# Layer 1: the second-level result goes up to the first level as float32 products on the two 64-row parts of the PE array

## The chip, the cores and the metric

The kernel runs on one core of a Trainium2 chip. The time is the device time of one execution in microseconds (us), as a median of several executions. The engines named below are PE (matrix products; its weight loads are listed apart as PEld), DVE (vector), ACT (scalar), POOL (GpSimd) and SP, whose queue issues the DMA transfers. SBUF is the on-chip memory of 128 partitions; PSUM holds the sums that PE writes, in banks.

## What is computed

The network has four layers, each `x = x + conv(group_norm(x))`, on 32 images of 96 channels and 56 x 56 pixels in float32. The change lies in layer 1, a wavelet convolution:

```python
def _L1_conv_ref(x, base_w, base_b, base_scale, wconv_w, wscale):
    ...  # 3 levels of a 2x2 Haar transform of x; at each level a depthwise
    ...  # 5x5 convolution of the four bands, scaled; then from the lowest
    ...  # level up: the inverse transform adds a level's low band to the
    ...  # level above; the base 5x5 convolution of x is added at the end
x = x + _L1_conv_ref(_gn(x), ...)
```

The kernel folds a level's transform, convolution and inverse transform into one depthwise filter on that level's low band. So there are three depthwise products: at full size (level 1, which also has the base convolution in it), on 2 x 2 sums (level 2) and on 4 x 4 sums (level 3). The result of level 3 is spread over 2 x 2 points and added to level 2, and the result of level 2 is spread and added to level 1. This last step is what the change touches.

## The kernel before

Layer 1 works channel by channel, two channels (a pair) per turn of its main loop, 48 pairs. A channel is held for all 32 images at once. Rows and a phase of the columns lie on 112 partitions, the upper and the lower half of the image (h = 0, 1) are two tiles, each with 14 columns of 32 images, 448 elements per partition. A halo of 16 rows fills partitions 112 to 127. A depthwise convolution along rows is then a product with a banded 128 x 112 matrix, one for each of three column shifts (sizes 448, 416 and 416).

The steps of a pair, each for the pair named (`i` is the pair that is finished, `nxt` the next one, `far` the one after), with the lines of the profile:

- `normal(far, j, h)`: DVE normalises a half image, L872 and L873.
- `matrices1`, `matrices2`: ACT brings loaded matrices into order, L748 and L776; the loads into `raw` have been issued by SP.
- `lowest1(nxt)`: eight weight loads and products on four 32-column strips of the array make the 2 x 2 sums (L887), ACT copies them to `x2` (L889). `lowest2(nxt)` makes the 4 x 4 sums likewise (L895, L897).
- `level3(nxt)`: five products on two 64 x 64 parts of the array (L903), and two ACT copies into `c3` (L904, L905).
- `level2(nxt, j)`: three products (L912) and one that adds `c3`, spread by the constant `up2` (L913), in one PSUM tile of 128 partitions x 224; partitions 0 to 55 belong to the upper half image, 64 to 119 to the lower. Then, for each half, ACT writes a rounded copy in the type float32r (L918), and DVE writes what the rounding left out (L919): the high part lies on partitions 0 to 55 of `c2`, the low part on partitions 64 to 119, so that one product over 128 partitions adds both.
- `level1(i, j, h)`: takes a PSUM tile `pf` (a pool of four), `coarse` adds the spread `c2` of this half by two products in float32r with weights `up1r` over all 128 rows (L930, 224 columns each, one for each column phase n), `fine` adds the three shifted products in float32 (L924), and DVE adds the residual into `y` (L943). After h = 1 the SP queue stores `y` (L950).

The pair 0 does `fine` in advance, in `begin`, and `coarse` last. PE, DVE, ACT and SP run their instructions in the order in which the code issues them. That order is written out by hand in the main loop:

```python
            do(lowest1, nxt)
            ...
            do(level1, i, 0, 0)
            do(lowest2, nxt)
            ...
            do(level1, i, 0, 1)
            do(level3, nxt)
            ...
            do(level1, i, 1, 0)
            do(level2, nxt, 0)
            do(level2, nxt, 1)
            do(matrices2, far, 1)
            do(level1, i, 1, 1)
```

On PE a turn is therefore: L887, L930, L924, L895, L930, L924, L903, L930, L924, L912, L913, L912, L913, L930, L924. From the twelfth pair on the SP queue also gets transfers for layer 2 (L1106, whole groups of 16 channels at a time; L1113 for the last 16 channels) among the loads (L736, L739: images; L766 to L768: matrices; L783: factors of the norm).

Of the kernel before, what the change touches and what calls it, by code (L numbers as in the profile page):

```python
# [10 lines left out]
F32 = mybir.dt.float32  # L11
BF16 = mybir.dt.bfloat16
F32R = mybir.dt.float32r
I16 = mybir.dt.int16
AF = mybir.ActivationFunctionType
ALU = mybir.AluOpType
# [4 lines left out]
B, C, H, W = 32, 96, 56, 56  # L21
# [8 lines left out]
W4 = W // NPH  # L30
HH = H // 2
PH = HH * NPH
# [596 lines left out]
NK = 3  # L629
LEN = 2 * (HH + HALO) - 1  # L630
MIDL = HH + HALO - 1
KW = 5
# [118 lines left out]
def shifts(n, ks):  # L751


    for d in sorted(range(-(ks // 2), ks // 2 + 1), key=abs):
        yield ks // 2 + d, slice(max(0, -d), n - max(0, d)), slice(max(0, d), n + min(0, d))
# [32 lines left out]
def layer1(ctx, tc, w, y0, left, made, norm, t1, t2, t3, y1, k2, behind):  # L788
# [4 lines left out]
    nc = tc.nc  # L793
    cp = ctx.enter_context(tc.tile_pool(name="l1c", bufs=1, reuse_waits="tile"))
# [3 lines left out]
    pfine = ctx.enter_context(tc.tile_pool(name="l1pf", bufs=4, space=PSUM, reuse_waits="tile"))  # L798
    psum = ctx.enter_context(tc.tile_pool(name="l1p", bufs=4, space=PSUM, reuse_waits="tile"))
    N2, N3 = W4 // 2, W4 // 2  # L800

    def constant(name, shape):
        t = cp.tile(shape, F32, tag=name, name=name)
        nc.sync.dma_start(t, w[name])
        return t

    def rounded(name, shape):

        t = cp.tile(shape, F32R, tag=f"{name}r", name=f"{name}r")
        nc.scalar.copy(t, constant(name, shape))  # L810
        return t

    NF = 3
    sets = [None] * NF
    for i in reversed(range(NF)):
        sets[i] = {
            name: cp.tile(shape, dtype, tag=f"{name}{i}", name=f"{name}{i}") for name, shape, dtype in (
                ("T3", [128, 64 * KW], F32), ("T2", [128, 2, NK, 128], F32), ("raw2", [128, 2, NK * PH], F32), ("c2", [128, 2, 2, N2, B], F32R),
                ("c3", [128, N3, B], F32))}
    for d in sets:  # L820
        for t in d.values():
            nc.gpsimd.memset(t.bitcast(F32) if t.dtype == F32R else t, 0.0)

    def load(i):

# [81 lines left out]
    def level2(st, j):  # L907


        ps = psum.tile([128, N2, B], F32, tag="w", name="pc2")  # L910
        for n, (k, to, of) in enumerate(shifts(N2, NK)):
            nc.tensor.matmul(ps[:, to], st["T2"][:, j, k, :], st["x2"][:, j, of], start=(n == 0), stop=False)  # L912
        nc.tensor.matmul(ps, up2[:, j, :], st["c3"], start=False, stop=True)  # L913
        n = PH // 2
        for h in range(2):
            high, low = (st["c2"][64 * i : 64 * i + n, j, h] for i in range(2))
            v = ps[64 * h : 64 * h + n]
            nc.scalar.copy(high, v)  # L918
            nc.vector.tensor_tensor(low, v, high, ALU.subtract)  # L919

    def fine(st, j, h, first):
        ps = st["pf"][j, h]
        for n, (k, to, of) in enumerate(shifts(W4, NK)):
            nc.tensor.matmul(ps[:PH, to], st["T"][j][:, h, k, :], st["x"][:, j, h, of],  # L924
                             start=first and n == 0, stop=not first and n == NK - 1)

    def coarse(st, j, h, first):
        ps, rows = st["pf"][j, h], slice(128 if first else PH)
        for n in range(2):
            nc.tensor.matmul(ps[rows, n::2, :], up1[:, h, n, rows], st["c2"][:, j, h],  # L930
                             start=first and n == 0, stop=not first and n == 1)

    def level1(st, j, h):
        if h == 0:
            st["y"] = io.tile([PH, 2, B, W4], F32, tag="y", name="y", bufs=3)
        if st["i"]:
            st["pf"][j, h] = pfine.tile([128, W4, B], F32, tag="f", name="pc1")
            coarse(st, j, h, True)
            fine(st, j, h, False)
        else:  # L940
            coarse(st, j, h, False)
        ps = st["pf"][j, h]
        nc.vector.scalar_tensor_tensor(  # L943
            st["y"][:, h], ps[:PH].rearrange("p q b -> p b q"), st["nr"][j][:PH, 2 * B : 2 * B + 1], st["X"][j][:PH, h],
            ALU.add, ALU.add)
        if h == 1:
            c = 2 * st["i"] + j
            if c >= C - GR:
                k2.straight(c, st["y"], 0)
            nc.sync.dma_start(y1[c // GR][c % GR].rearrange("(h p) b q -> p h (b q)", h=2),  # L950
                              st["y"].rearrange("p h b q -> p h (b q)"))
            if c >= C - GR:
                k2.straight(c, st["y"], 1)

    def begin(st):
        for j in range(2):
            matrices1(st, j)
        for j in range(2):
            matrices2(st, j)
        both = cp.tile([128, 2, 2 * B + 1], F32, tag="nr0", name="nr0")  # L960
        made.spread(both, pick, psum.tile([128, 2, 2 * B + 1], F32, tag="w", name="pr0"))
        st["nr"] = [both[:, j, :] for j in range(2)]
        for j in range(2):
            for h in range(2):
                normal(st, j, h)
                st["pf"][j, h] = pfine.tile([128, W4, B], F32, tag="f", name="pc1")
                fine(st, j, h, True)
# [3 lines left out]
    def do(step, i, *args):  # L971
        if i in sts:
            step(sts[i], *args)

    with tc.manual_schedule(engines=MANUAL_SP):
        low1 = constant("low1", [128, 2, 2, GC])
        up1 = rounded("up1", [128, 2, 2, 128])
        low2 = constant("low2", [128, GC])
        up2 = constant("up2", [128, 2, 128])
        pick = constant("pick", [C, 2, 128])  # L980
        for i in range(-3, PAIRS):
            nxt, far = i + 1, i + 2
            if i + 3 < PAIRS:
                sts[i + 3] = load(i + 3)
            if far == 0:
                begin(sts[0])
                continue
            do(lowest1, nxt)
            do(normal, far, 0, 0)
            do(matrices1, far, 0)  # L990
            do(normal, far, 0, 1)
            do(level1, i, 0, 0)
            do(lowest2, nxt)
            do(matrices2, far, 0)
            do(normal, far, 1, 0)
            do(level1, i, 0, 1)
            do(level3, nxt)
            do(matrices1, far, 1)
            do(normal, far, 1, 1)
# [5 lines that stand above are left out]
            sts.pop(i, None)  # L1005
            behind(i)
# [548 lines left out]
def lowest_bands():  # L1555

    low1 = np.zeros((PH + HALO * NPH, 2, 2, 128), np.float32)
    low2 = np.zeros((PH, 2, 2 * HH), np.float32)  # L1560
    up1 = np.zeros((128, 2, 2, 128), np.float32)
    up2 = np.zeros((2 * HH, 2, 128), np.float32)

    def at(r, p):
        return PH // 2 * (r // 14) + 14 * p + r % 14

    for r in range(HH):
        for p in range(NPH):
            for h in range(2):
                for n in range(2):  # L1570
                    low1[at(r, p), h, n, at(HH // 2 * h + r // 2, 2 * n + p // 2)] = 0.5
            for c in range(2):
                low2[at(r, p), c, HH * c + 2 * (r // 2) + p // 2] = 0.5
    n = PH // 2
    for i in range(2):
        for h in range(2):
            up1[64 * i : 64 * i + n, h, :, :PH] = low1[:PH, h, :, n * h : n * h + n].transpose(2, 1, 0)
        up2[:, :, 64 * i : 64 * i + n] = low2[n * i : n * i + n].transpose(2, 1, 0)


    def strips(v, axis):
        shape = v.shape[:axis] + (-1, HH) + v.shape[axis + 1 :]
        v = np.pad(v.reshape(shape), [(0, 4 * (a == axis + 1)) for a in range(v.ndim + 1)])
        return v.reshape(v.shape[:axis] + (-1,) + v.shape[axis + 2 :])

    of = [[low1[:, h, n, HH * (2 * h + n) : HH * (2 * h + n + 1)] for n in range(2)] for h in range(2)]
    low1 = strips(np.array(of).transpose(2, 0, 1, 3), 3)
    up2 = strips(up2, 0)
    return {"low1": low1, "low2": strips(strips(low2[:, 0, :HH], 0), 1), "up1": up1, "up2": np.concatenate([up2, up2])}


def layouts(a):
# [34 lines left out]
    def phase_taps(v):  # L1627
# [49 lines left out]
        "group": group.astype(np.float32),  # L1677
        "pick": np.repeat(np.eye(C, 2, dtype=np.float32)[:, :, None], 128, axis=2),
        **lowest_bands(),
        "grid": np.broadcast_to(grid, (C,) + grid.shape),  # L1680
    }
# [23 lines left out]
```

## Time and profile before

| | |
|---|---|
| median of three runs | 5628.25 us (5627.5 to 5648.81) |
| profiled execution | 5634.93 us, its span 5632.8 us |
| layer 1's products at full size (L924) | from 2685.5 to 3482 us of the span |
| L930, products of the step that is changed | 384, one record each |
| L918 on ACT, L919 on DVE | 192 each, median 341 and 390 ns |
| DMA share of the core's 16 engines, 3020 to 3180 us | 0.77 |

In the profile a float32 product stands as two records with a weight load each, a float32r product as one. The recorded duration of a product includes its way through the array, so that products that follow each other overlap in the records; how fast they follow is read from their starts, or from the chain of work that ended last, where every piece counts from the end of the one before it. That chain names, for each moment, the engine and line that set the time. In the list of instruction groups a form such as `64*64 64x224` means a part of the array of 64 rows and 64 columns and a moving tile of 64 partitions with 224 elements each.

### The profile page before, as it was taken

The page shows a single profiled execution, that of the slowest core. Times are in us where ns is not written, and L with a number is a line of the kernel's source. Part 1 is how long each engine was busy: PE and PEld are TensorE (multiplying, and loading weights), DVE is VectorE, ACT ScalarE, POOL GpSimd, SP SyncE. Part 2 cuts the span into 40 slices and gives each one's busy share as a digit, 9 for nine tenths or more (in the row PEclk, how much of TensorE's full clock was granted, in tenths as well). Part 3 has the DMA queues.
Part 4 walks back from the last instruction along what each step waited for, and adds up shares of the span by engine and source line. Part 5 has one row for each costly group of instructions (what it writes and reads, how often), then busy time and mean ns, then how long its engine had stood idle before and what let it go on. Part 6 is the DMA issues. An engine that isn't in the chain of part 4 may idle for free.

```text
span 5632.8 us, 138021 instructions
## 1 busy us (share of the span) xinstructions
PE 5379.4 (96%) x59896; PEld 2975.1 (53%) x59896; DVE 4589.1 (81%) x5317; ACT 4096.6 (73%) x5975; POOL 242.4 (4%) x164
## 2 busy tenths in 40 slices
PE   5999999999999999998899998999999999998999
PEld 2333333333333334333555555878787777776444
DVE  6999999999999999997666665777777777775777
ACT  5888888888888888885555554777777777676455
POOL 6000000000000000000000000000000000000000
PEclk9999999999999999998999998999999999999999
DMA  3023333322233222214677778296796796853888
GB/s 100 16 56 65 59 59 57 58 47 51 54 61 62 55 55 54 43 36 26 164 166 174 171 157 113 23 53 39 50 54 38 53 52 41 51 44 49 238 247 247
DMA packets 1291018, 455.86 MB, mean 81 GB/s; under 512 B 1105491, under 2 KB 1286483, under 8 KB 1288491
## 3 DMA queue, kind: packets, MB, share of 16 engines
q1 hardware_dynamic: 1290411, 447.03, 51.3%
q8 instruction: 470, 7.70, 0.6%
q14 instruction: 137, 1.12, 0.1%
HBM read 285.12 MB, written 214.08 MB: 89 GB/s over the span
## 4 chain that ended last, share of the span: by engine, by line
PE 78%; DMA 6%; ACT 5%; DVE 4%; SPq 3%; issue 2%; POOL 1%; ACTq 0%; DVEq 0%; POOLq 0%
PE psd L493 18%; PE psd L1276 13%; PE psj L548 11%; PE ps L426 8%; PE ps L1257 7%; PE pse L449 6%; PE pc L924 5%; PE psj L1319 4%; DMA X<-y 4%; ACT hi L1227 2%; PE pc L1451 2%; ACT u L1247 1%; PE pc L912 1%; DVE h L467 1%; ACT a L1247 1%
## 5 line engine op out<-in xcount | busy, mean ns | idle before, releaser
L467 DVE SCALAR_TENSOR_TENSOR h<-hpad,l_wdw,h 128x3136 f32<-128x3136 f32 x512 | 1782.3, 3481 | 9.1
L493 PE MATMUL psd<-plane,filt 128*32 128x392 f32 (+5 forms) x16384 | 1084.7, 485 | 0.0
L1276 PE MATMUL psd<-apad,diag 64*64 64x392 bf16 x20736 | 916.5, 330 | 75.0 <-issue 70.2
L1276 PEld LDWEIGHTS <-diag 64*64 64x64 bf16 x20736 | 688.4, 106 | 298.1 <-issue 121.2
L493 PEld LDWEIGHTS psd<-plane,filt 128*32 128x32 f32 (+1 forms) x16384 | 390.0, 108 | 675.4 <-issue 622.9
L748 ACT COPY T<-raw 128x112 f32<-128x112 f32 (+1 forms) x1386 | 445.9, 385 | 326.3 <-DMA raw<-tdiff 179.9
L1247 ACT ACTIVATE u<-ps,o,s 128x784 int16<-128x784 f32 x576 | 537.1, 1003 | 167.3 <-PE ps L1257 149.6
L1247 ACT ACTIVATE a<-psd,o,s 128x784 int16<-128x784 f32 x448 | 424.4, 1001 | 285.2 <-PE psd L1276 285.1
L426 PE MATMUL ps<-xn,l_wboth 96*128 96x392 f32 (+1 forms) x1536 | 465.6, 505 | 23.9 <-ACT xn L408 23.0
L467 DVE SCALAR_TENSOR_TENSOR hc<-hhalf,l_wdw,hc 128x1568 f32<-128x1568 f32 x256 | 473.7, 1850 | 16.2 <-ACT hc L460 9.5
L1257 PE MATMUL ps<-hi,l_w1q 96*128 96x392 f32 x1280 | 464.4, 363 | 6.6 <-DVE u L1245 3.7
L924 PE MATMUL pc<-x,T 128*112 128x416 f32 (+1 forms) x1152 | 451.3, 529 | 15.3 <-DVE x L873 15.3
L1257 PE MATMUL ps<-lo,l_w1q 96*128 96x392 f32 x1280 | 439.6, 343 | 3.9 <-DVE lo L1235 2.9
L1451 PE MATMUL pc<-x,T 128*112 128x416 f32 (+1 forms) x1152 | 418.6, 524 | 14.8 <-DVE x L1444 9.2
L449 PE MATMUL pse<-xn,l_wboth 96*32 96x392 f32 x4096 | 391.0, 500 | 3.2 <-ACT hab L470 3.2
L426 PEld LDWEIGHTS ps<-xn,l_wboth 96*128 96x128 f32 (+1 forms) x1536 | 219.2, 173 | 249.0 <-issue 54.1
L470 ACT ACTIVATE hab<-psd,o,s 128x784 f32<-128x784 f32 x256 | 284.3, 1115 | 58.4 <-PE psd L493 57.1
L1451 PEld LDWEIGHTS pc<-x,T 128*112 128x112 f32 x1152 | 202.8, 178 | 230.0 <-issue 185.4
L436 ACT ACTIVATE hpad<-ps,o,s 128x784 f32<-128x784 f32 x256 | 278.3, 1103 | 49.6 <-PE ps L426 48.0
L548 PE MATMUL psj<-h,wg 128*32 128x392 f32 x3072 | 307.2, 514 | 0.2 <-DVE wg L535 0.2
L548 PE MATMUL psj<-hab,wg 128*32 128x392 f32 x3072 | 305.6, 510 | 0.0
L924 PEld LDWEIGHTS pc<-x,T 128*112 128x112 f32 x1152 | 193.6, 180 | 163.6 <-issue 163.6
(263 smaller groups left out, 7254.9 us busy)
## 6 DMA issues: line engine op xcount, KB each, us to landing
X<-y SPq DMA_DIRECT2D x192, 392.0 KB
y<-xt SPq DMA_DIRECT2D x108, 392.0 KB
y<-y SPq DMA_DIRECT2D x96, 392.0 KB
out_dram<-y SPq DMA_DIRECT2D x96, 392.0 KB
twav<-zwav SPq DMA_DIRECT2D x768, 36.8 KB
y<-kept SPq DMA_DIRECT2D x72, 392.0 KB
xt<-y SPq DMA_DIRECT2D x59, 392.0 KB
xt<-in_x_dram SPq DMA_DIRECT2D x8, 2352.0 KB
```

The costliest lines, as they stand in the source:

```text
L426: nc.tensor.matmul(ps[p, j, :NT], wexp[:, k * 128 : k * 128 + 128][:, m], im["xn"][:, j, rows, :].rearrange("c h w -> c (h w)"), start=Tru ...
L449: nc.tensor.matmul(ps[f * GC : (f + 1) * GC, half, :NT].rearrange("p (r w) -> p r w", w=W2), wexp[:, c : c + GC], im["xn"][:, f % 2, r0 : ...
L467: nc.vector.scalar_tensor_tensor(h2, taken(im, k, t), wdw[:, k, t : t + 1], h2, ALU.mult, ALU.add)
L470: nc.scalar.activation(view, ps, AF.Silu, bias=bi[1][:, c : c + 1], scale=sc[1][:, c : c + 1], accum_out=accum)
L493: nc.tensor.matmul(ps[at * GC : (at + 1) * GC, r, :NT].rearrange("p (r w) -> p r w", w=W2)[:, r0 - half * n : r1 - half * n, q0:q1], filt[ ...
L548: nc.tensor.matmul(ps[s * GC : (s + 1) * GC, t, :NT].rearrange("c (m r q) -> c r q m", m=2, q=W4), wg[p, k, c * GC : (c + 1) * GC], phases ...
L748: nc.scalar.copy(to.rearrange("x t (p s) -> x t p s", p=NPH), v[:, k])
L924: nc.tensor.matmul(ps[:PH, to], st["T"][j][:, h, k, :], st["x"][:, j, h, of], start=first and n == 0, stop=not first and n == NK - 1)
L1247: nc.scalar.activation(out, ps, AF.Identity, bias=o[:, c : c + 1], scale=s[:, c : c + 1])
L1257: nc.tensor.matmul(ps[:, j, :NT], w1[:, k * 128 : k * 128 + 128], im[part][:, r0 : r0 + RT, :].rearrange("c h w -> c (h w)"), start=(part ...
L1276: nc.tensor.matmul(ps[q, j, :NT].rearrange("p (r w) -> p r w", w=W), diag[p, k, t, :], v, start=(t == 0), stop=(t == 8))
L1451: nc.tensor.matmul(ps[:, :, to], st["T"][:, h, k, :], st["x"][:, h, :, of], start=(n == 0), stop=(n == NK - 1))
```

## The change

`level2` copies its PSUM tile once, all 128 partitions in float32, by one ACT copy into a `c2` of half the size; the rounded copy, the subtraction on DVE and the type float32r are gone, and so are the constant's rounded copy (L810) and half of the constant. Partitions 0 to 63 of `c2` now hold the upper half image, 64 to 127 the lower. `coarse` is called once for both halves, at h = 0. It takes both PSUM tiles at once and issues four float32 products of 64 partitions, the upper half's on the array's rows 0 to 63 and the lower half's on rows 64 to 127, in turn. In the built program they have a part of 64 rows and all 128 columns, and each half writes its own PSUM tile.

```diff
-                ("T3", ...), ("c2", [128, 2, 2, N2, B], F32R),
+                ("T3", ...), ("c2", [128, 2, N2, B], F32),
...
         nc.tensor.matmul(ps, up2[:, j, :], st["c3"], start=False, stop=True)
-        n = PH // 2
-        for h in range(2):
-            high, low = (st["c2"][64 * i : 64 * i + n, j, h] for i in range(2))
-            v = ps[64 * h : 64 * h + n]
-            nc.scalar.copy(high, v)
-            nc.vector.tensor_tensor(low, v, high, ALU.subtract)
+        nc.scalar.copy(st["c2"][:, j], ps)
...
-    def coarse(st, j, h, first):
-        ps, rows = st["pf"][j, h], slice(128 if first else PH)
+    def coarse(st, j, first):
+        rows = slice(128 if first else PH)
         for n in range(2):
-            nc.tensor.matmul(ps[rows, n::2, :], up1[:, h, n, rows], st["c2"][:, j, h],
-                             start=first and n == 0, stop=not first and n == 1)
+            for h in range(2):
+                half = slice(64 * h, 64 * h + 64)
+                nc.tensor.matmul(st["pf"][j, h][rows, n::2, :], up1[half, n, rows], st["c2"][half, j],
+                                 start=first and n == 0, stop=not first and n == 1)

     def level1(st, j, h):
...
         if st["i"]:
-            st["pf"][j, h] = pfine.tile([128, W4, B], F32, tag="f", name="pc1")
-            coarse(st, j, h, True)
+            if h == 0:
+                for n in range(2):
+                    st["pf"][j, n] = pfine.tile([128, W4, B], F32, tag="f", name="pc1")
+                coarse(st, j, True)
             fine(st, j, h, False)
-        else:
-            coarse(st, j, h, False)
+        elif h == 0:
+            coarse(st, j, False)
...
-        up1 = rounded("up1", [128, 2, 2, 128])
+        up1 = constant("up1", [128, 2, 128])
```

On PE a turn becomes: L887, coarse (both halves), L924, L895, L924, L903, coarse (both halves), L924, L912, L913, L912, L913, L924. All other steps keep their order on every engine.

More of the change, by code (lines that the diff above doesn't have):

```diff
@@ L805, in constant @@
         return t
[L807 to L811, printed above, removed]
     NF = 3
@@ L817, in layer1 @@
             name: cp.tile(shape, dtype, tag=f"{name}{i}", name=f"{name}{i}") for name, shape, dtype in (
-                ("T3", [128, 64 * KW], F32), ("T2", [128, 2, NK, 128], F32), ("raw2", [128, 2, NK * PH], F32), ("c2", [128, 2, 2, N2, B], F32R),
+                ("T3", [128, 64 * KW], F32), ("T2", [128, 2, NK, 128], F32), ("raw2", [128, 2, NK * PH], F32), ("c2", [128, 2, N2, B], F32),
                 ("c3", [128, N3, B], F32))}
@@ L821, in layer1 @@
         for t in d.values():
-            nc.gpsimd.memset(t.bitcast(F32) if t.dtype == F32R else t, 0.0)
+            nc.gpsimd.memset(t, 0.0)
     def load(i):
@@ L1588, in lowest_bands @@
     up2 = strips(up2, 0)
-    return {"low1": low1, "low2": strips(strips(low2[:, 0, :HH], 0), 1), "up1": up1, "up2": np.concatenate([up2, up2])}
+    return {"low1": low1, "low2": strips(strips(low2[:, 0, :HH], 0), 1),
+            "up1": np.concatenate([up1[:64, 0], up1[64:, 1]]), "up2": np.concatenate([up2, up2])}
 def layouts(a):
```

## The prediction

> **What bounds the kernel now.** First the busy times of the page, to see which engines can matter at all:
>
> ```profile
> PE 5379.4 (96%) x59896; PEld 2975.1 (53%) x59896; DVE 4589.1 (81%) x5317; ACT 4096.6 (73%) x5975; POOL 242.4 (4%) x164
> ```
>
> PE leads, but this is an average over four layers, so the second view is the chain of waits inside layer 1. Its columns are start, length and what; one turn of the pair loop reads:
>
> ```profile
> 3019.81 0.41 PE pc L930 x2
> 3020.22 2.15 PE pc L924 x6
> 3022.37 1.17 PE pc L903 x9
> 3023.54 0.41 PE pc L930 x2
> ...
> 3028.53 0.38 PE pc L913 x2
> 3028.91 0.21 PE pc L930 x2
> 3029.13 2.15 PE pc L924 x6
> 3031.28 0.89 PE pa L887 x8
> 3032.16 0.41 PE pc L930 x2
> 3032.58 2.15 PE pc L924 x6
> 3034.73 0.52 PE pa L895 x8
> 3035.25 0.41 PE pc L930 x2
> ```
>
> The reader is to see that nothing but PE is on it: 3035.25 - 3019.81 = 15.44 us a turn, and L887 comes back every 15.43 to 15.44 us in 36 of 47 turns. In that turn DVE is busy 10.4 and ACT 9.1 us. Second, the same pair of L930 costs 0.21 us after L913 and 0.41 after L887, L895 and L903. Those three use parts of the array, L913 and L924 all its rows and columns: leaving a tiling costs 0.20 us. Third, not all turns are like this. In the chain from 2860 to 3020 us:
>
> ```profile
> 2983.90 4.58 SPq L1106
> 2988.52 6.34 SPq L736
> ...
> 2996.84 5.49 DMA raw<-twav
> ...
> 3005.21 2.18 PE pc L903 x9
> ```
>
> Here the transfers for layer 2 hold up the loads, and PE is out of work until L903. By the starts of L887, five turns lose 7.8, 9.4, 2.0, 6.5 and 8.7 us over 15.44 so, and the last three full turns 1.1, 3.3 and 2.6: 41 us in all.
>
> **Prices on PE.** L924 is 6 records with 2 x (448 + 416 + 416) = 2560 columns in 2.15 us: 0.84 ns a column and record, so a float32 product of 224 columns is 2 x 0.188 us. The float32r product is one record at 0.21 / 2 = 0.107 us. Entering a tiling: L887 streams 2 x 448 columns in four strips at once, 0.75 us, and takes 0.89; L895 0.376 of 0.52; entry 0.14. What that consists of shows the timeline of PE and PEld (start, busy time, line, form):
>
> ```profile
> 3021.51 0.86 PE L924 MATMUL pc<-x,T 128*112 128x416 f32 x2
> 3022.30 0.46 PE L903 MATMUL pc<-x,T 64*64 64x224 f32 x2
> ```
>
> The second of the two L924 starts 0.35 after the first, at 3021.86, and has streamed at 3022.21; L903 begins at 3022.30. So 0.09 us of empty array, and then a weight load that nothing hides. A load of 128 columns takes 0.107 (the two L930 loads after a change start 0.108 apart), one of 112 columns about 0.10, by columns.
>
> **Do two row parts run at once?** L903 has five products: 224, 192 and 160 columns on rows 0 to 63, 192 and 160 on rows 64 to 127. One after the other they are 2 x 928 x 0.84 = 1.56 us, the first part alone 2 x 576 x 0.84 = 0.97; with an entry of 0.20 the latter gives the 1.17 of the chain. So they overlap fully. But L903's parts write different partitions of PSUM, the changed products the same partitions of two tiles. For that the nearest row is L493 of layer 0, whose 64-row products write the same strips in two banks: 16384 records of some 385 columns (0.32 us) make 5300 us, four at a time 1325, and the page has 1084.7 busy. Half of the records are 64*32; these must run eight at a time. I take full overlap.
>
> **Are the 64-row loads hidden under products?** The new form (64 rows, 128 columns, float32) is not in the trace. The rows:
>
> ```profile
> L493 PEld LDWEIGHTS psd<-plane,filt 128*32 128x32 f32 x1628 | 49.6, 110 | 87.0 <-issue 83.7 <-ACT plane L453 3.3
> ...
> L493 PEld LDWEIGHTS psd<-plane,filt 64*32 64x32 f32 x1616 | 27.4, 105 | 45.9 <-issue 38.9
> ...
> L426 PEld LDWEIGHTS ps<-xn,l_wboth 96*64 96x64 f32 x96 | 6.4, 136 | 10.5 <-issue 6.7 <-ACT gate L529 3.8
> ```
>
> and, from the list of L903 (minimum, median and longest ns),
>
> ```profile
> L903 PEld LDWEIGHTS pc<-x,T x480: 182/186/228, 2701.5 to 3465.0; 64*64 64x64 f32 x160
> ```
>
> Loads of 32 columns cost the same with 64 rows as with 128; but 64 columns take 186 ns in L903 and 136 in L426. 50 ns more for 64 columns would be 100 more for 128: 0.207 instead of 0.107, longer than the 0.188 that hides it. L903's weights are read with a step of five elements (`T3[tile, k::KW]`), L493's and the new ones without a step, so I take 0.107, hidden from the second record on; the upper end is for the range.
>
> The TensorE page of the Trainium skill (TensorE: Matmul & The Clock Gate, Part 3, "The mechanism") speaks against it: a weight load overlaps running products only when it goes to another group of rows. In this trace L912 issues 224- and 192-column records in a row, all on 128 rows, six in 1.03 us, which is their 2 x 608 columns at 0.84 ns and leaves no room for a load, so the measurement decides. By the rule three more loads would show in each coarse step, about 2 x 3 x 0.107 = 0.64 us a turn, and the time would be some 30 us above my sum.
>
> **The change, part by part, per turn.** Removed: L930, 0.41 + 0.41 + 0.41 + 0.21 = 1.44 us. Added: coarse after L887 and after L903, each: empty array and first load 0.20, four records on each part at once 4 x 0.188 = 0.75, leaving again with the first L924 load 0.20, together 1.15; twice, 2.30. Kept: L895 to L924 is still a change, 0.20. L913 to L924 has none any more: 0. Sum 2.50, so +1.06 us a turn; 47 turns +49.8. In the last pair nothing stands between: 2 x 1.15 instead of 4 x 0.21, +1.5. Together +51 us.
>
> Off the path: 192 casts of 341 ns on ACT become 96 copies of 128x224 (347 ns, as L897): -32 us of ACT; 192 x 390 ns = -75 us of DVE. That gains nothing in a turn of 15.44 us, where DVE idles 5 us. Where PE waited for this pair of steps, it does: the waits of L930 for L919 come to 8.0 us, 12 times, and in two of the last turns the chain runs through L918 and L919; I take -3, and keep 0 and -8 as the ends. The second half's `pf` tile is now needed one L924 earlier. It is freed by L943 of the pair before, which in DVE's order stands ahead of this turn's L872, where DVE waits for loads; so no new wait for PE, whose queue behind it is all of the turn. No DMA is issued in another place; the constant's load halves, and its 0.6 us cast goes, before layer 1's products start.
>
> Given back in the stalls: there PE waits for a chain of transfers that starts at L943 of the turn before, about a turn of PE work earlier. It takes in the 1.06 of one turn, at the five places -5.3 and in the last three turns -3.2.
>
> Sum: 51 - 3 - 8.5 = +40 us. On the profiled execution that is 5634.9 + 40 = 5675; the median run is 6.7 us below that execution, so 5628.25 + 40 = 5668.
>
> **Rivals.** (A) The parts do not overlap. For: the new pairing has never run here. Against: L903 and L493. The streams cost 0.75 more, twice a turn: +1.06 + 1.50 = 2.56, 47 turns 120, +3 for the last pair, less 3 and some 18 in the stalls (2.56 at most places, no more than there is): +102, 5730. 8%. (B) The loads bind, at 0.207: (0.10 for the first, 3 x 0.02 for the rest) x 2 = +0.32 a turn, +15 us, 5683; with loads wholly exposed and of that length, 2 x (0.10 + 3 x 0.207) = 1.4 a turn, 5735 at the utmost, which I hold for remote. For: L903's 186. Against: L493's 105. 12%. (C) The other side: DVE with ACT bounds the loop and PE only fills the time. Then 4 x 0.39 us of L919 go from every turn: 47 x 1.56 = 73 less, 5555. It decides if DVE's work and waits in a turn exceed PE's. For: DVE waits 2.1 us for L918 in the turn shown. Against: 10.4 busy of 15.44, and no DVE piece in the chain of a steady turn. 3%. (D) The stalls give back much more than a turn's 1.06: if all 41 us went, +51 - 41 - 3 = +7, 5635; half of it, 5652. For: three quarters of the DMA engines' time is used in a steady turn and less would be in a longer one. Against: the stall's chain is the transfers' own length. 11%.
>
> **How the numbers follow.** The forecast has 66%, its own range 5656 to 5680. A measurement of this kernel can tell 0.5%, 28 us, from no change, so "same" ends at 5656: D and a slice (8%) of the rest, 19%; slower 78%; faster, C, 3%. The range leaves out A and C, and reaches over D's middle to the upper part of B: 5640 to 5705.
>
> **What would show it.** In the chain of the changed kernel a turn of about 16.5 us; coarse pieces of about 1.1 us (8 records) after L887 and L903; L924 right after L913. Products of the two halves starting some 10 ns apart show the overlap; 1.9 us pieces show A; starts 0.21 apart on one part instead of 0.19 show B. If turns are still 15.4 us, the price of changing the tiling or of float32r was read wrongly. If the turns are right and the sum is not, the stalls are where to look.

## The result, and the profile after

| | before | changed | ratio, 95% interval |
|---|---|---|---|
| median of 17 runs each | 5629.17 us | 5655.77 us | 1.0044 (1.0034 to 1.0053) |
| span of the profiled execution | 5632.8 us | 5657.9 us | |

By the ratio the change costs 25 us, 0.44% (19 to 30 us). The forecast was +40 us and 5668. The measured 5655.77 lies on the forecast side and in the range of 5640 to 5705, but just below the forecast's own 5656 to 5680, and so within the 0.5% that was called no change, to which the prediction gave 19% (78% to slower).

The busy times of the changed kernel:

```profile
PE 5424.8 (96%) x60280; PEld 2995.2 (53%) x60280; DVE 4516.3 (80%) x5125; ACT 4060.7 (72%) x5878; POOL 240.1 (4%) x164
```

DVE has 192 instructions and 73 us less, ACT 36 us less, and PE is 45 us busier: the work has gone from the two engines with idle time to the one without. The chain of waits in a steady turn (start, length, what). Lines have moved in the changed file: L881, L889 and L897 are the former L887, L895 and L903, L906 and L907 the former L912 and L913, L913 the former L924, and L921 is the new coarse product.

```profile
3021.52 0.89 PE pa L881 x8
3022.41 0.96 PE pc L921 x8
3023.36 2.33 PE pc L913 x6
3025.70 0.52 PE pa L889 x8
3026.21 2.33 PE pc L913 x6
3028.54 1.17 PE pc L897 x9
3029.72 0.96 PE pc L921 x8
3030.67 2.33 PE pc L913 x6
...
3035.44 0.38 PE pc L907 x2
3035.82 2.15 PE pc L913 x6
3037.97 0.89 PE pa L881 x8
```

Again only PE, and the turn is 3037.97 - 3021.52 = 16.45 us, 1.01 more than before. The full-size products take 2.33 us instead of 2.15 where they follow a tiling (after L921 and L889): 0.18 for leaving it, which stood in L930's pieces before. After L907 they take 2.15. A coarse step is 0.96 + 0.18 = 1.14 us. Its loads and products, from the list of L921 (minimum, median and longest ns) and from the timeline of PE (start, busy time):

```profile
L921 PEld LDWEIGHTS pc<-c,up x768: 169/187/333, 2704.4 to 3502.9; 64*128 64x128 f32 x188, 64*112 64x112 f32 x4
L921 PE MATMUL pc<-c,up x768: 349/349/738, 2704.4 to 3503.1; 64*128 64x224 f32 x188, 64*112 64x224 f32 x4
```

```profile
3022.34 1.03 PE L921 MATMUL pc<-c,up 64*128 64x224 f32 x8
3023.29 0.63 PE L913 MATMUL pc<-x,T 128*112 128x448 f32 x1
```

Eight records of 0.188 us of streaming, 1.5 us in a row, are over 0.95 us after the first begins, with the first load and the empty array at the end in it: the two parts run at once. A load lasts 187 ns, as the 190 of a full 128 x 128 load, and not 100 ns more, as L903's slow loads of half as many columns would have had it.

Where the 25.1 us of the two spans lie, by the starts of L887 (L881), the first product of each turn:

| | before | changed | difference |
|---|---|---|---|
| first turn begins at | 2697.2 | 2695.0 | -2.2 |
| first two turns, which fill the pipeline | 23.2 | 19.9 | -3.3 |
| 45 turns at the steady length (15.44, 16.45) | 694.8 | 740.3 | +45.5 |
| what these turns lose beyond it | 41.6 | 25.4 | -16.2 |
| from the last L887 to the end | 2176.1 | 2177.3 | +1.2 |

So PE's price was forecast well (+1.06 a turn against +1.01), and what the stalls give back was not. That the last line comes out near the forecast's +1.5 is luck: it holds layer 2, whose depthwise products (L1276 in the kernel before, the same in every kernel here) take from 1627 to 1664 us, from the first to the last, in the profiled executions of this document.

### The profile page after: what moved, and what is told of

It reads as the page before. It is cut to its first block, busy times and chain, and to the rows that moved or that the text cites. A ratio compares the mean times of both kernels' runs of the same rounds, so it can differ in the third digit from the quotient of the medians.

```text
span 5657.9 us, 138455 instructions
## 1 busy us (share of the span) xinstructions
PE 5424.8 (96%) x60280; PEld 2995.2 (53%) x60280; DVE 4516.3 (80%) x5125; ACT 4060.7 (72%) x5878; POOL 240.1 (4%) x164
## 4 chain that ended last, share of the span: by engine, by line
PE 77%; DMA 8%; ACT 5%; DVE 4%; SPq 3%; issue 2%; POOL 1%; ACTq 0%; DVEq 0%; POOLq 0%
PE psd L493 18%; PE psd L1269 13%; PE psj L548 11%; PE ps L426 8%; PE ps L1250 7%; PE pse L449 6%; PE pc L913 6%; DMA X<-y 4%; PE psj L1312 3%; DMA raw<-tdiff 2%; ACT hi L1220 2%; ACT u L1240 1%; PE pc L906 1%; DVE h L467 1%; PE pc L921 1%
## 5 line engine op out<-in xcount | busy, mean ns | idle before, releaser
L913 PE MATMUL pc<-x,T 128*112 128x416 f32 (+1 forms) x1152 | 459.7, 536 | 14.7 <-DVE x L867 14.7
L936 DVE SCALAR_TENSOR_TENSOR y<-pc,nr,X 112x448 f32<-112x448 f32 x192 | 130.8, 683 | 320.6 <-PE pc L913 273.7
L1444 PEld LDWEIGHTS pc<-x,T 128*112 128x112 f32 x1152 | 203.3, 178 | 230.7 <-issue 188.2
```

What stands on the lines that cost most here:

```text
L1444: nc.tensor.matmul(ps[:, :, to], st["T"][:, h, k, :], st["x"][:, h, :, of], start=(n == 0), stop=(n == NK - 1))
```

## The experiments

Two theories for the 16 us: a longer turn lets the transfers for layer 2 (L1106) catch up ("lead"), or the work taken off ACT and DVE shortens the waits. "Stalls" below is the fourth line of the table, what the 45 turns lose beyond the steady length, always of one profiled execution.

**The changed kernel once more.**

> The changed kernel once more, for how much its stalls vary from one execution to the next. Both theories: a steady turn of 16.45 us and about +25 us over before. The eight turns that stalled lost 25.4 us beyond a steady turn in the changed kernel and 41.8 before; if the difference of 16 is real, this run's stalls lie at 20 to 30 us; if it is chance from one execution to the next, they may as well be 35 to 45.

Measured: turn 16.45, stalls 20.5, ratio to before 1.0048 (1.0029 to 1.0067). The stalls are small in a second execution too.

**Little work on ACT and DVE, the old price on PE.**

```diff
-("c2", [128, 2, N2, B], F32)
+("c2", [128, 2, N2, B], F32R)
...
-up1 = constant("up1", [128, 2, 128])
+up1 = rounded("up1", [128, 2, 128])
```

> The changed kernel with c2 and up1 rounded to float32r and no low part, so this step's sum is coarser. PE then pays about what it paid before: two parts at 0.107 x 2 plus 0.20 in and 0.20 out, 0.61 us twice and 0.20 once, 1.42 us a turn instead of 1.44; a turn of 15.4 us. ACT and DVE have as little work as in the changed kernel. Lead theory (the stalls shrink because a longer turn gives the transfers more time): stalls as before, 42 us, time 0 to 3 us below before. Rival (the stalls and the first turns shrink because ACT's casts and DVE's subtractions are gone): stalls near 25 to 30 us and the first two turns shorter, 10 to 18 us below before.

Measured: turn 15.36, stalls 47.3, ratio 1.0010 (0.9997 to 1.0023). With ACT and DVE relieved as in the changed kernel and a turn as short as before, the stalls are as before. That is against the rival. Only the first two turns are shorter, as the rival had it (21.0 us against 23.2); more on these below.

**The old work on ACT and DVE, the new price on PE.**

```diff
+    spare = cp.tile([128, N2, B], F32, tag="spare", name="spare")
...
-        nc.scalar.copy(st["c2"][:, j], ps)
+        n = PH // 2
+        for h in range(2):
+            v = slice(64 * h, 64 * h + n)
+            nc.scalar.copy(st["c2"][v, j], ps[v])
+            nc.vector.tensor_tensor(spare[v], ps[v], st["c2"][v, j], ALU.subtract)
```

> The changed kernel with the old work of ACT and DVE put back: two copies of 56 partitions per channel and two subtractions into a spare tile that nobody reads; products as changed. A turn of 16.45 us by both. Lead theory: stalls as in the changed kernel, 25 us, and its time, +25 us over before. Rival: stalls near 35 us and longer first turns, +33 to +40 us over before.

Measured: turn 16.45, stalls 21.3, ratio 1.0041 (1.0025 to 1.0056). In the groups of a turn of this kernel the old work is back (L913 and L914 are its copies and subtractions):

```profile
L914 DVE TENSOR_TENSOR spare<-pc,c 56x224 f32<-56x224 f32 x4 | 1.6, 389 | 2.1 <-ACT c L913 2.1
L913 ACT COPY c<-pc 56x224 f32<-56x224 f32 x4 | 1.4, 339 | 3.1 <-PE pc L909 2.2 <-DVE spare L914 0.9
```

The time is that of the changed kernel. What the change saves on DVE and ACT, 73 and 36 us of busy time by the page, is worth nothing within the 7 to 9 us that these intervals resolve.

**The kernel before without the subtraction.**

```diff
-            nc.vector.tensor_tensor(low, v, high, ALU.subtract)
```

> The kernel before without DVE's subtraction (L919); the low part in c2 stays zero, so this step's sum is coarser. PE's instructions are all there: a turn of 15.44 us. Lead theory: 0 to 3 us below before, stalls 40 us. Rival: DVE's 4 x 0.39 us a turn and the turns of ACT and DVE waiting for each other are gone, stalls nearer 32 us, 8 to 12 us below before.

Measured: turn 15.44, stalls 39.0, ratio 0.9997 (0.9982 to 1.0011). The same from the other side: 1.6 us of DVE a turn taken away, and no gain that the interval (-10 to +6 us) shows.

**A longer turn alone.**

```diff
         ps = psum.tile([128, N2, B], F32, tag="w", name="pc2")
+        for _ in range(1 + j):
+            nc.tensor.matmul(ps, st["T2"][:, j, NK // 2, :], st["x2"][:, j], start=True, stop=True)
```

> The kernel before with three more float32 products of 224 columns on PE per turn (level 2 repeats its first product, whose sum the real one then starts anew, once for j = 0 and twice for j = 1): 3 x 0.376 = 1.13 us, a turn of 16.57 us; ACT, DVE, transfers and the float32r step as before. Lead theory (only the length of the turn shrinks the stalls): stalls 18 to 25 us instead of 39 to 42, so about +30 us over before. If something else of the changed kernel shrank them (its order on PE, its smaller c2): stalls of 33 us or more, since only one turn's 1.13 is taken from each of eight, and about +42 us over before.

Measured: turn 16.57, stalls 26.8, ratio 1.0032 (1.0019 to 1.0046). The stalls shrink as in the changed kernel although nothing of the change is in it. 26.8 is just outside the 18 to 25 of the lead theory and clearly below the 33 of its rival; with the executions of the changed kernel at 25.4 and 20.5 I count it for the former. The time fits neither: +18 us (11 to 26), where the one said +30 and the other +42. In the profiled execution the last turn of the loop begins 37.8 us later than in the kernel before, but layer 2's depthwise products are the shortest of all, 1627 us (1661 in the kernel before). Whether the other executions were as short there, and why, isn't shown. So it is the stalls that speak for the lead theory here, not the time.

**Each half on its own.**

```diff
-            if h == 0:
-                for n in range(2):
-                    st["pf"][j, n] = pfine.tile([128, W4, B], F32, tag="f", name="pc1")
-                coarse(st, j, True)
+            st["pf"][j, h] = pfine.tile([128, W4, B], F32, tag="f", name="pc1")
+            coarse(st, j, h, True)
...  # coarse issues the products of the half h alone
```

> The changed kernel with one coarse step for each half, as before the change, in float32 on 64 rows: four times 0.20 + 4 x 0.188 + 0.20 = 1.15 us instead of 1.44 us in all, a turn of 18.6 us (+3.16). If the price were only the streams and entering were free in it, 17 us. Lead theory: stalls near 10 us or less, about +148 - 35 = +110 us over before.

Measured: turn 18.52, no stalls at all (0.0), ratio 1.0163 (1.0138 to 1.0188), +92 us. Its chain:

```profile
3030.41 0.95 PE pc L921 x4
3031.36 2.33 PE pc L913 x6
3033.69 0.89 PE pa L881 x8
3034.58 0.95 PE pc L921 x4
3035.53 2.33 PE pc L913 x6
```

Four records take as long alone (0.95) as eight on two parts (0.96): the second half image is free. Taking both halves together is worth 18.52 - 16.45 = 2.07 us a turn. And the price of entering and leaving, 0.2 each, holds in a kernel it was not read from. The forecast of its time, +110, was too high: the stalls gave back all of their 42 us and not 35, and the turn was 0.1 shorter than computed, which is 11 of the 18 us.

**The order of the four products.**

```diff
-        for n in range(2):
-            for h in range(2):
+        for h in range(2):
+            for n in range(2):
```

> The changed kernel with the loops over n and h in the other order: both products of the upper half, then both of the lower. If PE hands out records strictly in order, the lower half's first record waits for the upper half's last to start: 3 x 0.188 = 0.56 us more per coarse step, a turn of 17.6 us, about +45 to +55 us over before. If each row part has its own queue that reads ahead, 16.45 us and the time of the changed kernel, about +25.

Measured: turn 16.46, coarse still 0.96 in the chain, stalls 24.1, ratio 1.0044 (1.0025 to 1.0063). The order doesn't matter: also when one half's products all stand first in the code, the records start in pairs, 13 ns apart in a pair (7 in the changed kernel). On one part alone records follow 189 ns apart (halves apart), so the two of a pair are on different parts. Across the parts, then, PE doesn't hold to the order of the code that the description of the kernel before gives for it.

**High and low parts on the two row parts.**

```diff
-        nc.scalar.copy(st["c2"][:, j], ps)
+        high, low = (st["c2"][:, j, i] for i in range(2))
+        nc.scalar.copy(high, ps)
+        nc.vector.tensor_tensor(low, ps, high, ALU.subtract)
...
         for n in range(2):
+            for i in range(2):
                 ...  # products of up1 (float32r) with c2[half, j, i]
```

> Both half images together on the row parts, but with float32r high and low parts: one ACT cast and one DVE subtraction of 128 x 224 per channel, and four products of 0.107 on each part: 0.20 + 0.43 + 0.20 = 0.83 us twice and 0.20 once, 1.86 us a turn instead of 1.44, a turn of 15.86 us. With stalls of some 34 us by the lead theory: +20 - 8 = about +12 us over before, 13 less than the changed kernel. If loads of 0.107 can't be hidden under products of 0.107 on two parts at once: up to 0.83 more a turn.

Measured: turn 15.81, stalls 40.1, ratio 1.0007 (0.9989 to 1.0024), +4 us. Its coarse steps in the chain (L930 here):

```profile
3036.88 0.64 PE pc L930 x8
3037.52 2.33 PE pc L921 x6
3039.85 0.52 PE pa L895 x8
```

0.64 = 0.20 + 4 x 0.11: a record with a new load of 128 columns starts every 0.11 us on each part, on both at once, so the loads don't add to the 0.107 us of a product. This form computes what the kernel before does, with half as many instructions on ACT and DVE in this step, and is not measurably slower. On PE float32 costs 16.45 - 15.81 = 0.64 us a turn against it.

**The transfers for layer 2 in small pieces.**

```diff
-        for g in range(self.begun, channels // GR):
-            for i, pair in enumerate(self.pairs):
-                self.nc.sync.dma_start(pair[g * GR : (g + 1) * GR], self.y1[g][:, :, 2 * i : 2 * i + 2, :])
-            self.begun = g + 1
+        c = self.begun
+        n = min(4, channels - c, GR - c % GR)
+        if n > 0:
+            for i, pair in enumerate(self.pairs):
+                self.nc.sync.dma_start(pair[c : c + n], self.y1[c // GR][c % GR : c % GR + n, :, 2 * i : 2 * i + 2, :])
+            self.begun = c + n
...
-                    k2.begin(min(2 * pair, C - GR))
+                    k2.begin(min(2 * pair - 2, C - GR))
```

The last line holds the pieces back by one more pair.

> The kernel before with the same transfers for layer 2 (L1106), but at most 4 channels of them per turn instead of 16 at a time. If these bursts make the stalls, the turns at which they stood are 15.44 us like the others, stalls 5 to 18 us (the last turns' own remain), and the time 20 to 35 us below before. If the DMA engines are short of time as such, the stalls move and keep their 40 us, time as before.

> The changed kernel with the same spreading. With the bursts gone there is little for a longer turn to give back: the changed kernel's price stands nearly in full, 47 x 1.01 = 47 us, 35 to 45 us over the spread kernel before instead of 25; so 5 to 20 us above the kernel before. If the give-back did not come from the bursts, it stays 25 over the spread kernel before.

Measured: ratios to the kernel before 1.0268 (1.0247 to 1.0289) for the kernel before so spread, +151 us, and 1.0304 (1.0283 to 1.0326) for the changed kernel so spread. Both expectations fail: a piece of 4 channels holds up the loads about as long as one of 16, and the changed kernel lies some 20 us above the other, neither the 35 to 45 of the one theory nor clearly the 25 of the other. The chain of the spread kernel before in one of its long turns (L1108 issues the pieces):

```profile
3062.08 4.70 SPq L1108
3066.82 12.62 DMA X<-y
...
3087.94 4.01 SPq L1108
```

In this kernel all nine turns that follow a piece of 4 are lengthened so, in the changed one all but the first. But these turns show the point more plainly than was planned. In the windows view (stretch, its length, busy time of PE, PEld, DVE, ACT, POOL, granted clock, share of the DMA engines, GB/s), one such turn of the spread kernel before and one of the spread changed kernel:

```profile
3062.00:3089.20 27.20, 16.76 (x73) 9.37 (x72) 10.13 (x16) 8.86 (x28) 0.00 (x0) 0.81 0.62 115
```

```profile
2962.40:2989.80 27.40, 19.41 (x83) 10.78 (x82) 8.59 (x12) 8.46 (x26) 0.00 (x0) 0.81 0.58 104
```

The eight long turns in a row are 27.2 us in the mean in the one (26.6 to 27.8) and 27.5 in the other (25.2 to 29.2), 0.3 apart where the steady turns are 1.01 apart. Over all turns it is plainer. The twelve turns ahead of the first piece's stall are 185.6 us in the one and 197.4 in the other, PE's price in full. The 33 turns from there to the last are 707.7 and 706.6 us: where transfers set the turn, PE's dearer step costs nothing.

**The two transfers of a burst in two turns.**

```diff
+        g, i = self.begun // 2, self.begun % 2
+        if g < channels // GR:
+            self.nc.sync.dma_start(self.pairs[i][g * GR : (g + 1) * GR], self.y1[g][:, :, 2 * i : 2 * i + 2, :])
+            self.begun += 1
```

> The kernel before with the same transfers for layer 2 in pieces of 16 channels, but one of the two (L1106) in one turn and the other in the next, since a piece of 4 channels held SP and the loads behind it about as long as one of 16. If a stall is what one turn's slack doesn't cover, two half bursts with a turn's slack each cost less: stalls 15 to 28 us instead of 42, the time 10 to 25 us below before, below both kernels. If each piece costs a stall of its own, they stay at 40 or more.

> The changed kernel with the same split. Lead theory: fewer stalls leave less to give back, so it lies further above the split kernel before than the 25 us of the unsplit pair: 30 to 42 us, and about 10 us above the kernel before. If the give-back has another source, 25 over the split kernel before.

Measured: ratios to the kernel before 0.9981 (0.9969 to 0.9994) and 1.0037 (1.0024 to 1.0049); stalls 42.4 and 21.7. The split kernel before is the only one measurably faster than both kernels of the case, by 11 us (3 to 17) over the one before, at the lower edge of what was expected. But the reason given for it fails: 15 to 28 us of stalls were expected, and its profiled execution has those of before, in other turns. What that execution is shorter by lies behind the last turn, where executions differ anyway, so where the 11 us come from isn't shown. The two split kernels lie 0.56% apart, some 31 us; the intervals are too wide to tell that from 25.

## Why the prediction was right, and where it was off

**Turn length against stalls.** All kernels whose transfers were left as they were, one execution each:

| kernel | turn, us | stalls, us |
|---|---|---|
| float32r on the parts, no low part | 15.36 | 47.3 |
| before | 15.44 | 41.6 |
| before, no subtraction | 15.44 | 39.0 |
| high and low on the parts | 15.81 | 40.1 |
| changed; once more; with the old work on ACT and DVE | 16.45 | 25.4, 20.5, 21.3 |
| changed, other order | 16.46 | 24.1 |
| before with a longer turn | 16.57 | 26.8 |
| halves apart | 18.52 | 0.0 |

The stalls follow the turn's length, whatever ACT and DVE have to do and however PE spends the turn. From 15.4 to 16.5 us they fall from about 42 to about 23.

**PE's prices** held. Changing the tiling (0.20 to enter and 0.18 to leave), the overlap of the parts, and loads hidden from the second record on were all read from rows of layer 1 and layer 0 and gave +1.06 a turn; measured +1.01, the rest being some 0.02 on each departure from a tiling. Rival A (no overlap) and B (loads that bind) are out by the chain and by L921's load rows.

**ACT and DVE off the path** held: no gain in two runs, where -3 was taken and 0 to -8 kept; the runs resolve 8 us, so the -3 itself is neither shown nor excluded. **Rival C**, 73 us faster, fell with it.

**The step that was mis-sized** is "It takes in the 1.06 of one turn, at the five places -5.3 and in the last three turns -3.2". Measured in its place: -16.2, and -21.1 by the second execution of the changed kernel, so that a part of rival D (the stalls give back more than a turn's worth) came true. For half of D the prediction has 5652; its own sum, 51 less half of 41 less 3, gives 5656, and that is what was measured. The premise was a chain that begins at one L943 and ends a turn of PE work later, so that only the turn between could help.

Place by place the miss is narrower than the sum. The stalls of the traced executions lie at the turns 14, 19, 27 and 35 (counted from 0; each follows a burst of transfers for layer 2) and in the last four full turns, 43 to 46, of which the first follows a burst too. The means of the four kernels with short turns (15.36 to 15.81 us) and of the five executions with long ones (16.45 to 16.57):

| place | short turns, us | long turns, us | given back | forecast |
|---|---|---|---|---|
| turn 14 | 9.3 | 1.8 | 7.5 | 1.06 |
| turn 19 | 10.5 | 8.5 | 2.0 | 1.06 |
| turn 27 | 3.9 | 1.4 | 2.5 | 1.06 |
| turn 35 | 4.0 | 0.6 | 3.3 | 1.06 |
| turns 43 to 46 | 14.3 | 11.3 | 3.0 | 4.3 |

So the price by one turn was about right for the last four turns and too small at the other four places, above all at the first. The windows view shows that place. First the kernel before, then the changed one: a turn ahead of the first burst, the burst's turn, and the stalled one, with the columns given above:

```profile
2875.10:2890.50 15.40, 15.40 (x77) 9.00 (x76) 11.45 (x25) 9.17 (x28) 0.00 (x0) 1.00 0.65 174
2890.50:2905.90 15.40, 15.40 (x75) 9.02 (x74) 11.45 (x25) 9.17 (x28) 0.00 (x0) 1.00 1.08 131
2905.90:2929.10 23.20, 18.41 (x75) 10.27 (x74) 10.16 (x16) 8.77 (x28) 0.00 (x0) 0.85 0.81 152
```

```profile
2879.40:2895.80 16.40, 16.40 (x83) 9.45 (x82) 9.87 (x21) 8.47 (x26) 0.00 (x0) 1.00 0.62 166
2895.80:2912.30 16.50, 16.50 (x87) 9.52 (x88) 9.87 (x21) 8.48 (x26) 0.00 (x0) 1.00 1.27 109
2912.30:2932.50 20.20, 18.11 (x83) 10.05 (x82) 8.60 (x12) 8.47 (x26) 0.00 (x0) 0.92 0.74 161
```

The reader is to look at the DMA share times the length, over the burst's turn and the next together: 15.4 x 1.08 + 23.2 x 0.81 = 35.4 us of all 16 engines before, 16.5 x 1.27 + 20.2 x 0.74 = 35.9 after (a share above 1 must count packet times that reach beyond the stretch, so only the sum is used). The same transfers, near the whole length of the two turns, 38.6 and 36.7 us. A reading of this is that the transfers of a burst set two turns and not one, so that the PE work of both is hidden; then the two turns together would be as long in every kernel. Turn 19 with the one before it fits: 41.5 us in the mean of the short-turn kernels and 41.5 in that of the long-turn ones. The last four turns fit too, 77.4 us together before and 76.5 after. The first burst doesn't: its two turns take 38.7 to 41.8 us in the short-turn kernels and 33.3 to 36.7 in the long-turn ones, so it gave back more than two turns' worth. Nor does the kernel with the halves apart: its turns of 18.52 us have no stall at all, so turn 19 with the one before is 37.0 us and the last four are 74.1, shorter than what the transfers would set by this reading. So the size of what is given back is measured, and why it is that size stays open. A second error of the same kind: the table of turns lay open, and a price by "one turn" should have had its bound from the other side, the 41.6 us that there were to give.

**The first turns** gave -5.5 us where the prediction had two turns' price, +2.1. The end of the second turn lies at 2719.4 to 2721.9 us in the executions of the kernels built on the one before, and at 2714.9 to 2720.8 in those built on the changed one. Two of the latter, with the transfers for layer 2 spread and split, have the changed kernel's instructions in these turns and end them at 2719.4 and 2720.8, where the changed kernel itself has 2714.9 twice. So the gain is not one that the change always brings, and what decides it isn't settled.

In the sum: by the profiles, the 45 turns +45.5 where +47.7 was forecast, the stalls -16.2 where -11.5 was, the first turns -5.5 where +2.1 was, and the end +1.2 where +1.5 was: +25 instead of +40.

## What to carry to other kernels

Where an engine fills every turn of a loop, price a change on that engine alone, with tiling changes and exposed weight loads counted one by one; 109 us of savings on two engines that idle were worth nothing measurable here. Before the turns are multiplied, set apart those that something else sets: a dearer step cost nothing in the 33 turns where that was so, and a longer turn can give back more than its own length at a burst of transfers (7.5 us at the first one, for turns about 1 us longer). Two row parts of the array run two sets of products in the time of one, 2.07 us a turn here, but entering and leaving the tiling cost 0.2 us each. Float32r with high and low parts stays 0.64 us a turn cheaper on them than float32.

## What was not expected of the hardware

The two row parts don't need their products in turn: with all of one half first, the coarse step stays at 0.96 us. Float32r products of 107 ns ran on both parts at once with a new 128-column load for each record, at 0.11 us a record. And of the two transfers of a burst the second, which writes 4 partitions of 224 runs of 112 bytes, took as long to issue as one that writes 16 (4.70 us in the spread kernel, 4.58 in the kernel before), and the chain then waited 12.6 us for the load behind it. No run shows why.
